# Turning a feed-forward layer's inputs on VectorE and through DRAM instead of on TensorE

## The chip, the core and the metric

The kernel runs on one core of a Trainium2 chip. TensorE (PE) multiplies matrices, VectorE (DVE) and ScalarE (ACT) work element by element, GpSimd (POOL) makes index tables and issues indirect DMAs, and SyncE (SP) issues the large DMAs. Each engine takes its instructions in order[...]. An engine waits on semaphores that other engines and DMAs raise. The metric is the device time of one execution in microseconds (us), taken as the median of several runs.

## What is computed

The input x has 4 x 512 = 2048 rows (tokens) of 512 numbers, in f32. Every token has a number that selects one of four experts, and every expert is one 512 x 512 matrix. The first half adds a gated expert product to x, the second half adds a gated feed-forward layer (FFN).

```
x = x + tanh(g_xattn) * moe(layernorm(x), ids, ctx, ctx, ctx)
x = x + tanh(g_ffn) * ffn(layernorm(x), w1, w3, w2, wr)

def moe(h, ids, Wg, Wu, Wd):          # E = 4
    expert = min(ids // 6250, 3)
    y_e = (silu(h @ Wg[e].T) * (h @ Wu[e].T)) @ Wd[e].T
    return y of the token's own expert

def ffn(h, w1, w3, w2, wr):
    gates = top 2 of softmax(h @ wr.T), normalised      # 8 routes
    h = silu(silu(h @ w1.T) @ w3.T) @ w2.T
    out = zeros_like(h)
    for k in range(2):
        out = out.at[index_k].add(gate_k * h)           # index_k is 0 to 7
    return out
```

The FFN's output lands in rows 0 to 7 of the result alone, since the indices of the routes, 0 to 7, are used as row numbers. All 2048 tokens contribute to these eight rows, so every token still goes through both FFN layers and the routing.

## The kernel before

**Tiles.** Tokens are sorted by expert on the chip. The sorted tokens make 17 passes of 128 rows: passes 0 to 12 (NF = 13) hold tokens of one expert, and passes 13 to 16 hold remainders, in four groups of Q = 32 rows with an expert for each group. `order` (L389) is the order in which passes are run: 0, 1, 2, 3, 4, 5, NF, 6, 7, 8, NF+1, 9, 10, NF+2, 11, 12, NF+3.

**One pass, first half.** `gather` (L393) fetches the rows of x with an indirect DMA on POOL. `load` (L436) reads the expert's number into a register on SP and issues the DMA of its matrix, 1 MB. A full pass loads one matrix, a remainder pass four. The matrices lie in the pool "mp" of seven buffers, so a load waits until the matrix seven places earlier in the order of loads has been used for the last time. `centre` (L403) takes mean and variance and subtracts the mean on DVE; `scale` (L409) makes the inverse root there. `turn_in` (L413) transposes the tile on PE (four transposes of 128 x 128) and ACT copies it out. `up` multiplies by the matrix (z, L459), with ACT's silu and DVE's product (g, L473) behind it. `turn_mid` transposes g, and `down` multiplies again (y, L459) and adds to x on DVE (L487); POOL scatters x to the output. `norms` (L498) normalises the new x for the FFN, into h_f.

**To the FFN.** `turn_out` (L516) transposes h_f on PE ("tp_f", four transposes), and ACT copies the result into `hT2`, one tile for each FFN half of 1024 tokens. A half of the FFN starts when its last pass is turned: `sums_of_hT` (L597) makes the logits of the routing for each half of 512 columns ("lg", L705, 64 small matmuls in all) and, on DVE, four sums T1 to T4 of the half's quarters; T1 is the difference of the two column halves. `turned` (L714) transposes the logits on DVE. `first_layer` then runs a scheme of seven block products in place of eight ("X", "Y", "Z", L628), and `second_layer` the product with w3 ("v", L736) and the gated sums.

**Order.** The order is written out by hand: the program's order is the order on each engine. The loop at L878 runs i from 2 to 18. An iteration puts on PE: `up` of order[i], `turn_in` of order[i+1], `down` of order[i-1], `turn_out` of order[i-2], a `step` of a running FFN, `turn_mid` of order[i]. It also issues `gather` and `load` of order[i+3]. FFN half 0 begins at the end of i = 10, because order[8] is pass 7.

**Start.** Before the first pass the kernel makes tables on DVE: `from_row` (rows to gather), `which0` and `matrix_table(0, 2)` (experts of the first two passes). The table for the other passes, `matrix_table(2, NU)`, and `row_tables` (L311) follow after the first two tiles are centred. `which1` (L847) is a copy on POOL behind the first gather, which makes the second load wait for that gather. PE runs 31 matmuls without a use ("idle", `busy`) during this time.

Of the kernel before, what the change touches and what calls it, by code (L numbers as in the profile page):

```python
# [25 lines left out]
def tile_gated_moe_ffn(  # L26
# [59 lines left out]
    xp = ctx.enter_context(tc.tile_pool(name="xp", bufs=5))  # L86
    work = ctx.enter_context(tc.tile_pool(name="work", bufs=3))
    small = ctx.enter_context(tc.tile_pool(name="small", bufs=4))
    ps_mm = ctx.enter_context(tc.tile_pool(name="ps_mm", bufs=2, space=bass.MemoryType.PSUM))
    ps_x = ctx.enter_context(tc.tile_pool(name="ps_x", bufs=2, space=bass.MemoryType.PSUM))  # L90
    ps_y = ctx.enter_context(tc.tile_pool(name="ps_y", bufs=1, space=bass.MemoryType.PSUM))
# [189 lines left out]
    later = ct_([P, 2 * E, NU], F32, "later")  # L281
    stepped = ct_([P, 2 * E - 1, NU], F32, "stepped")

    def matrix_table(n0, n1):
        n = n1 - n0
        nc.vector.tensor_tensor(
            later[:, :, n0:n1],
            place0[:, n0:n1].unsqueeze(1).to_broadcast([P, 2 * E, n]),
            cut[:, 1 : 2 * E + 1].unsqueeze(2).to_broadcast([P, 2 * E, n]),
            ALU.is_ge,  # L290
        )
        nc.vector.tensor_tensor(
            stepped[:, :, n0:n1],
            later[:, 0 : 2 * E - 1, n0:n1],
            steps.unsqueeze(2).to_broadcast([P, 2 * E - 1, n]),
            ALU.mult,
        )
        with nc.allow_low_precision("whole numbers below 4096"):
            nc.vector.tensor_reduce(
                which[:, n0:n1], stepped[:, :, n0:n1].rearrange("p e n -> p n e"), AX.X, ALU.add  # L300
            )

    busy(21)
    from_row = ct_([P, NP], I32, "from_row")
    nc.vector.tensor_scalar(from_row, tok, -1.0, 0.0, ALU.add, ALU.max)
    matrix_table(0, 2)

    first = ct_([P, NU - NF], I32, "first")
    to_row = ct_([P, NP], I32, "to_row")
# [1 line left out]
    def row_tables():  # L311

        pad = ct_([P, NP], F32, "pad")
        nc.vector.tensor_scalar(pad, tok, 1.0, float(4 * NT), ALU.is_lt, ALU.mult)
        nc.vector.scalar_tensor_tensor(to_row, tok, -1.0, pad, ALU.add, ALU.add)

        pads = ct_([P, E], F32, "pads")
        nc.vector.tensor_sub(pads, size[:, 2, :], num[:, 0, :])
        behind = ct_([P, E, NU - NF], F32, "behind")
        nc.vector.tensor_tensor(  # L320
            behind,
            later[:, E : 2 * E, NF:NU],
            pads.unsqueeze(2).to_broadcast([P, E, NU - NF]),
            ALU.mult,
        )
        psum = ct_([P, NU - NF], F32, "psum")
        nc.vector.tensor_reduce(psum, behind.rearrange("p e n -> p n e"), AX.X, ALU.add)
        nc.vector.tensor_sub(psum, place0[:, NF:NU], psum)
        nc.vector.tensor_scalar(
            first, psum, float(-(NB - 1) * TB), float(TB), ALU.add, ALU.min  # L330
        )


    hT2 = [ct_([P, KC, TB + (Q if b == NB - 1 else 0)], F32, f"hT2_{b}") for b in range(NB)]
    s1 = ct_([P, KC, TB], F32, "s1")
    acc = ps_acc.tile([P, D], F32, tag="acc", name="acc")
    accT = ps_acc.tile([P, KC, NR], F32, tag="acc", name="accT")
# [98 lines left out]
    def load(p):  # L436

        n0, n = (p, 1) if p < NF else (NF + (p - NF) * G, G)
        mats[p] = []
        for i in range(n0, n0 + n):  # L440
            at = nc.values_load(
                early[i] if i in early else which[0:1, i : i + 1],
                engines=[SP],
                min_val=0,
                max_val=(E - 1) * D,
                skip_runtime_bounds_check_because="an expert's number, times D",
            )
            m = mp.tile([P, KC, D], F32, tag="m", name=f"m_{i}")
            nc.sync.dma_start(m, ctxT[bass.ds(at, D), :].rearrange("(k p) f -> p k f", p=P))
            mats[p].append(m)  # L450
# [47 lines left out]
    def norms(p_in, p_out):  # L498
# [14 lines left out]
        if p_in is not None:  # L513
            rss[p_in] = rs[-1]

    def turn_out(p):  # L516

        tp = transposed(hs2.pop(p), f"f{p}").rearrange("p (k t) -> p k t", k=KC)
        if p < NF:
            b, t = divmod(p, TB // P)  # L520
            nc.scalar.copy(hT2[b][:, :, t * P : (t + 1) * P], tp)  # L521
            return
        for i in range(G):
            n = (p - NF) * G + i
            place = NF * P + n * Q - (NB - 1) * TB
            at = nc.values_load(
                first[0:1, n : n + 1],
                engines=[ACT],
                min_val=min(place - E * (Q - 1), TB),
                max_val=min(place, TB),  # L530
                skip_runtime_bounds_check_because="its place less at most E (Q - 1) pads, at most TB",
            )
            nc.scalar.copy(hT2[NB - 1][:, :, bass.ds(at, Q)], tp[:, :, i * Q : (i + 1) * Q])

    def route(b, lt):

# [60 lines left out]
    def sums_of_hT(b):  # L597


        lgs = [logits(b, half) for half in range(2)]  # L600
        b11, b12 = hT2[b][:, 0:2, 0:HB], hT2[b][:, 0:2, HB:TB]
        b21, b22 = hT2[b][:, 2:4, 0:HB], hT2[b][:, 2:4, HB:TB]
        ts = [ffp.tile([P, 2, HB], F32, tag=f"T{i}", name=f"T{i}_{b}") for i in range(1, 5)]
        nc.vector.tensor_sub(ts[0], b12, b11)
        lts[b] = [turned(b, half, lg) for half, lg in enumerate(lgs)]
        nc.vector.tensor_sub(ts[1], b22, ts[0])
        nc.vector.tensor_sub(ts[2], b22, b12)
        nc.vector.tensor_sub(ts[3], b21, ts[1])
        return b11, b21, b22, ts

    def first_layer(b):
# [14 lines left out]
        def product(out_ps, a, bb, c, start):  # L626
            for k in range(2):
                nc.tensor.matmul(  # L628
                    out_ps,
                    a[:, k, c * P : (c + 1) * P],  # L630
                    bb[:, k, :],
                    start=start and k == 0,
                    stop=k == 1,
                    skip_group_check=True,
                )
# [62 lines left out]
    def logits(b, half):  # L698


        lg = ps_x.tile([P, P], F32, tag="x", name=f"lg_{b}_{half}")
        for k in range(KC):
            cols = hT2[b][:, k, half * HB : (half + 1) * HB].rearrange("p (t c) -> p t c", t=TT)
            for i in range(P // Q):
                nc.tensor.matmul(  # L705
                    lg[i * Q : (i + 1) * Q, :],
                    wr[:, k, :],
                    cols[:, :, i * Q : (i + 1) * Q],
                    start=(k == 0),
                    stop=(k == KC - 1),  # L710
                )
        return lg
# [116 lines left out]

    SHORT = 1  # L830
    last = {b: max(i for i, p in enumerate(order) if min(p // (TB // P), NB - 1) == b) for b in range(NB)}
    running, hT_sums, lts, w1_sums = [], {}, {}, []

    def step():
        if running:
# [3 lines left out]
            if r in (0, SHORT):  # L839
                step()  # L840

    early = {order[0]: which0[0:1, :]}
    load(order[0])
    gather(order[0])

    which1 = ct_([P, 1], I32, "which1")
    nc.gpsimd.tensor_copy(which1[0:1, :], which[0:1, order[1] : order[1] + 1])  # L847
    early[order[1]] = which1[0:1, :]
    for i in range(1, 5):
        gather(order[i])  # L850
    load(order[1])
    nc.sync.dma_start(gates[:, 0:1], g_xattn.to_broadcast([P, 1]))
    nc.sync.dma_start(gates[:, 1:2], g_ffn.to_broadcast([P, 1]))
    first_in(order[0])
    centre(order[1])
    scale(order[0], order[1])
    matrix_table(2, NU)
    load(order[2])
    w1 = load_w(w1T, "w1")
    wr = load_w(wrT, "wr")  # L860
    load(order[3])
    row_tables()
    positions.close()
    ffp = ctx.enter_context(tc.tile_pool(name="ffp", bufs=1))
    up(order[0], inside=lambda: turn_in(order[1]))
    centre(order[2])
    scale(order[2])
# [5 lines left out]
    turn_mid(order[1])  # L873
    norms(order[3], order[0])
    load(order[4])
    summing = sums_of_w1()
    owed = []
    for i in range(2, NP + 2):  # L878
        if i < NP:
            up(order[i])  # L880
        if i + 1 < NP:
            turn_in(order[i + 1])
        if i + 2 < NP:
            centre(order[i + 2])
        if i + 3 < NP:
            gather(order[i + 3])
            load(order[i + 3])
        if i <= NP:
            down(order[i - 1])
        turn_out(order[i - 2])  # L890
        if i <= NP:
            norms(order[i + 2] if i + 2 < NP else None, order[i - 1])
        step()
        if i > NP:
            step()
        if 5 <= i < 9:
            next(summing)
        if i == 7:
            w3 = load_w(w3T, "w3")
            w2 = load_w(w2T, "w2")  # L900
        if i < NP:
            turn_mid(order[i])
        for b in range(NB):
            if last[b] == i - 2:
                hT_sums[b] = sums_of_hT(b)
                running.append(ffn(b))
        if last[0] != i - 2:
            step()
    fetched = False
    while running:  # L910
        step()
# [50 lines left out]
```

## Time and profile before

| | |
|---|---|
| time, median of three runs | 278.3 us (278.0 to 278.48) |
| the profiled execution | 278.8 us |
| its span, first to last instruction | 277.1 us |
| granted TensorE clock | 0.998 |
| four transposes "tp_f" of one turn_out, in the chain | 0.44 us |
| ACT copy of one turn_out (L521) | 586 ns |
| DVE transpose 128x128 of the logits (L716) | 304 ns |
| DVE 128x512 scalar_tensor_tensor (L473, L487) | 749 ns |
| moved by DMA | 42.54 MB, mean 154 GB/s |

The span is what the profiler sees of one execution, and the execution's own time is 1.7 us longer. Durations in the profile are those of this one execution. A line such as `109.60 3.57 PE y L459 x32` in the chain says: at 109.60 us from the start, for 3.57 us, PE ran 32 matmuls of line 459 that write y. A matmul of f32 appears as two instructions, so a full pass has 8 where the program has 4, and a remainder pass 32. "SPq" is the queue on which SP issues DMAs: the time beside it is that of the issue, not of the transfer. The trace leaves buffer numbers out of names (m, z, y), so passes are told apart by their time and their count of matmuls.

### The profile page before, as it was taken

The page shows a single profiled execution, that of the slowest core. Times are in us where ns is not written, and L with a number is a line of the kernel's source. Part 1 is how long each engine was busy: PE and PEld are TensorE (multiplying, and loading weights), DVE is VectorE, ACT ScalarE, POOL GpSimd, SP SyncE. Part 2 cuts the span into 40 slices and gives each one's busy share as a digit, 9 for nine tenths or more (in the row PEclk, how much of TensorE's full clock was granted, in tenths as well). Part 3 has the DMA queues.
Part 4 walks back from the last instruction along what each step waited for, and adds up shares of the span by engine and source line. Part 5 has one row for each costly group of instructions (what it writes and reads, how often), then busy time and mean ns, then how long its engine had stood idle before and what let it go on. Part 6 is the DMA issues. An engine that isn't in the chain of part 4 may idle for free.

```text
span 277.1 us, 3564 instructions
## 1 busy us (share of the span) xinstructions
PE 267.2 (96%) x1173; PEld 125.2 (45%) x1173; DVE 147.3 (53%) x596; ACT 69.2 (25%) x134; POOL 39.1 (14%) x62
## 2 busy tenths in 40 slices
PE   5888999999999999999999999999999999999994
PEld 2443555553454445444344344534345444444362
DVE  6369877777977769927354392516352620711000
ACT  2022222322322322124133132312113233311120
POOL 5510122221222102311110010101010000000000
PEclk9999999999999999999999999999999999999999
DMA  0775999656759998498305085001000000000000
GB/s 1 231 260 202 383 391 392 237 195 222 222 181 392 393 392 323 139 384 275 145 10 180 2 289 200 38 0 40 1 11 2 0 0 1 0 0 2 0 0 2
DMA packets 20722, 42.54 MB, mean 154 GB/s; under 512 B 2143, under 2 KB 2207, under 8 KB 20704
## 3 DMA queue, kind: packets, MB, share of 16 engines
q1 hardware_dynamic: 17952, 33.66, 34.4%
q0 software_dynamic: 2720, 8.65, 8.7%
q8 instruction: 9, 0.15, 0.2%
q14 instruction: 9, 0.07, 0.1%
q10 hardware_dynamic: 32, 0.01, 0.0%
HBM read 38.10 MB, written 4.47 MB: 154 GB/s over the span
## 4 chain that ended last, share of the span: by engine, by line
PE 91%; DVE 4%; DMA 3%; issue 1%; POOL 0%; DVEq 0%
PE y L459 21%; PE v L736 20%; PE z L459 19%; PE X L628 10%; PE Y L628 5%; PE tp_f L386 3%; PE tp_g L386 3%; PE tp_a L386 3%; PE Z L628 2%; DMA x<-in_x_dram,from_row 2%; PE acc L748 1%; PE lg L705 1%; PE accT L764 1%; DMA idt<-in_ids_dram 1%; PE o L820 0%
## 5 line engine op out<-in xcount | busy, mean ns | idle before, releaser
L459 PE MATMUL z<-m,hT 128*32 128x512 f32 (+1 forms) x232 | 61.8, 595 | 0.2 <-ACT hT L434 0.2
L459 PE MATMUL y<-m,gT 128*32 128x512 f32 (+1 forms) x232 | 61.4, 594 | 0.0
L736 PE MATMUL v<-w,s 128*128 128x512 f32 (+1 forms) x136 | 57.3, 570 | 0.0
L736 PEld LDWEIGHTS v<-w,s 128*128 128x128 f32 x136 | 25.0, 190 | 27.2 <-issue 26.7
L459 PEld LDWEIGHTS z<-m,hT 128*32 128x32 f32 (+1 forms) x232 | 22.6, 146 | 29.4 <-issue 28.1
L459 PEld LDWEIGHTS y<-m,gT 128*32 128x32 f32 (+1 forms) x232 | 22.6, 146 | 27.8 <-issue 27.8
L488 POOL DMA_INDIRECT out_dram<-x,to_row x17 | 17.2, 1010 | 87.6 <-DVE x L487 85.4
L395 POOL DMA_INDIRECT x<-in_x_dram,from_row x17 | 16.8, 989 | 76.2 <-DVE h_a L407 36.1
L473 DVE SCALAR_TENSOR_TENSOR g<-z,rs_a,g 128x512 f32<-128x512 f32 x17 | 12.7, 749 | 25.7 <-ACT g L472 25.7
L472 ACT ACTIVATE g<-z,rs_a 128x512 f32<-128x512 f32 x17 | 11.7, 688 | 51.2 <-PE z L459 50.7
L487 DVE SCALAR_TENSOR_TENSOR x<-y,tg,x 128x512 f32<-128x512 f32 x17 | 12.7, 749 | 17.3 <-PE y L459 17.3
L744 ACT ACTIVATE s<-v 128x512 f32<-128x512 f32 (+1 forms) x17 | 9.7, 572 | 41.9 <-PE v L736 41.9
L521 ACT COPY hT<-tp_f 128x512 f32<-128x512 f32 x13 | 7.6, 586 | 43.5 <-PE tp_f L386 43.5
L346 DVE BATCH_NORM_STATS2 st_a<-x 128x6 f32<-128x512 f32 x16 | 11.0, 688 | 9.9 <-DMA x<-in_x_dram,from_row 9.9
L628 PE MATMUL X<-T,S 128*128 128x512 f32 x32 | 15.0, 592 | 0.0
L386 PEld LDWEIGHTS tp_f<-ident,h_f 128*128 128x128 f32 x68 | 8.2, 141 | 10.2 <-issue 10.2
L386 PEld LDWEIGHTS tp_a<-ident,h_a 128*128 128x128 f32 x64 | 7.6, 141 | 10.2 <-issue 9.6
L346 DVE BATCH_NORM_STATS2 st_f<-x 128x6 f32<-128x512 f32 x17 | 11.8, 695 | 0.6
L479 ACT COPY gT<-tp_g 128x512 f32<-128x512 f32 x17 | 10.0, 586 | 8.0 <-PE tp_g L386 8.0
L646 DVE TENSOR_TENSOR s<-X,c 128x512 f32<-128x512 f32 x4 | 2.8, 692 | 16.2 <-PE X L628 16.2
L386 PE MATMUL tp_g<-ident,g 128*128 128x128 f32 x68 | 10.2, 273 | 1.0 <-DVE g L473 1.0
L386 PEld LDWEIGHTS tp_g<-ident,g 128*128 128x128 f32 x68 | 8.2, 141 | 5.5 <-issue 5.2
(164 smaller groups left out, 273.4 us busy)
## 6 DMA issues: line engine op xcount, KB each, us to landing
m<-in_ctxT_dram SPq DMA_DIRECT2D x29, 1024.0 KB
w<-in_w1T_dram SPq DMA_DIRECT2D x1, 1024.0 KB
w<-in_w3T_dram SPq DMA_DIRECT2D x1, 1024.0 KB
w<-in_w2T_dram SPq DMA_DIRECT2D x1, 1024.0 KB
x<-in_x_dram,from_row POOLq DMA_INDIRECT x17, 6.1
out_dram<-x,to_row POOLq DMA_INDIRECT x17, 6.1
wr<-in_wrT_dram SPq DMA_DIRECT2D x1, 64.0 KB
x_first<-out_dram SPq DMA_DIRECT2D x4, 4.0 KB
```

The lines of the kernel that those rows point to most:

```text
L346: nc.vector.bn_stats(st, xt)
L386: nc.tensor.transpose(tp[:, k * P : (k + 1) * P], h[:, k * P : (k + 1) * P], ident)
L395: nc.gpsimd.indirect_dma_start(out=xt, out_offset=None, in_=x, in_offset=bass.IndirectOffsetOnAxis(ap=from_row[:, p : p + 1], axis=0),)
L459: nc.tensor.matmul(out_ps[i * n : (i + 1) * n, :], lhs[:, k * P + i * n : k * P + (i + 1) * n], m[:, k, :], start=(k == 0), stop=(k == KC ...
L472: nc.scalar.activation(g, z, AF.Silu, scale=rs)
L473: nc.vector.scalar_tensor_tensor(g, z, rs, g, ALU.mult, ALU.mult)
L479: nc.scalar.copy(gT, tp)
L487: nc.vector.scalar_tensor_tensor(xt, y, tg[:, 0:1], xt, ALU.mult, ALU.add)
L488: nc.gpsimd.indirect_dma_start(out=out, out_offset=bass.IndirectOffsetOnAxis(ap=to_row[:, p : p + 1], axis=0), in_=xt, in_offset=None, bou ...
L628: nc.tensor.matmul(out_ps, a[:, k, c * P : (c + 1) * P], bb[:, k, :], start=start and k == 0, stop=k == 1, skip_group_check=True,)
L736: nc.tensor.matmul(v, s1[:, k, c_b + t * P : c_b + (t + 1) * P], w3[:, k, c0 : c0 + n], start=(k == 0), stop=(k == KC - 1),)
L744: nc.scalar.activation(s2, v, AF.Silu)
```

## The change

Passes 0 to 11 are no longer transposed on PE. Four of them make a set. `set_turned` transposes each 32x32 block of h_f on DVE and writes it to the set's own tile (`hT2[b]`, now one tile for each set, and one for the rest). After the fourth pass of a set, SP issues a DMA that copies the tile, 1 MB, to a buffer in DRAM. `fetch_turned`, called one iteration later, issues four DMAs of 256 KB that read it back, so that each block comes to the partitions of its column; columns are then in another order within the set. Passes 12 to 16 keep the transposes on PE. `set_turned` and `fetch_turned` stand behind `norms` in the loop. FFN half 0 begins one iteration later, at the end of i = 11, and a `step` now follows each iteration without the old exception.

The tables are made in one piece, and all of them ahead of the first gather in the program's order. `held` takes the place of `which1`: POOL copies the experts' numbers to it in two parts, one behind the first gather and one behind the fifth, and the loads read it. `scale(order[0])` stands ahead of `centre(order[1])`. The two loads of gates move behind the third matrix, and w1 and wr are loaded at i = 2.

```diff
-    def matrix_table(n0, n1):
...
-    matrix_table(0, 2)
+    nc.vector.tensor_tensor(
+        later,
+        place0.unsqueeze(1).to_broadcast([P, 2 * E, NU]),
+        cut[:, 1 : 2 * E + 1].unsqueeze(2).to_broadcast([P, 2 * E, NU]),
+        ALU.is_ge,
+    )
...
-    hT2 = [ct_([P, KC, TB + (Q if b == NB - 1 else 0)], F32, f"hT2_{b}") for b in range(NB)]
+    NS = NF // 4 * 4
+    assert NS == (NB * 2 - 1) * TT and E * (Q - 1) <= NF * P - NS * P
+    hT2 = [ct_([P, G, KC, P], F32, f"hT2_{b}") for b in range(NB * 2 - 1)]
+    hT2.append(ct_([P, KC, HB + Q], F32, "hT2_last"))
+
+    def inputs(b):
+        if b < NB * 2 - 1:
+            return hT2[b].rearrange("p g k c -> p k g c")
+        return hT2[b][:, :, 0:HB].rearrange("p k (g c) -> p k g c", g=TT)
...
+    def set_turned(p):
+        b, i = divmod(p, 4)
+        place = hT2[b]
+        h = hs2.pop(p)
+        nc.vector.transpose(
+            place.rearrange("p q k (i t) -> p k q i t", i=4)[:, :, :, i, :],
+            h.rearrange("p (k q t) -> p k q t", k=KC, q=4),
+        )
+        if i == 3:
+            copy = dram.tile([P, 4, KC * P], F32, tag=f"copy{b}", name=f"copy_{b}")
+            nc.sync.dma_start(copy, place.rearrange("p q k c -> p q (k c)"))
+            turning.append((place, copy))
+
+    def fetch_turned():
+        for place, copy in turning:
+            for q in range(4):
+                nc.sync.dma_start(
+                    place[q * Q : (q + 1) * Q].rearrange("f g k c -> f g (k c)"),
+                    copy[:, q, :].rearrange("(g f) c -> f g c", g=4),
+                )
+        turning.clear()
...
-        b11, b12 = hT2[b][:, 0:2, 0:HB], hT2[b][:, 0:2, HB:TB]
-        b21, b22 = hT2[b][:, 2:4, 0:HB], hT2[b][:, 2:4, HB:TB]
+        left, right = inputs(2 * b), inputs(2 * b + 1)
+        b11, b12, b21, b22 = left[:, 0:2], right[:, 0:2], left[:, 2:4], right[:, 2:4]
...
-            cols = hT2[b][:, k, half * HB : (half + 1) * HB].rearrange("p (t c) -> p t c", t=TT)
+            cols = inputs(2 * b + half)[:, k]
...
     row_tables()
     positions.close()
     ffp = ctx.enter_context(tc.tile_pool(name="ffp", bufs=1))
+    held = ct_([P, NU], I32, "held")
...
+    load(order[0])
+    gather(order[0])
+    one = slice(order[1], order[1] + 1)
+    nc.gpsimd.tensor_copy(held[0:1, one], which[0:1, one])
+    load(order[1])
+    for i in range(1, 5):
+        gather(order[i])
+    rest = slice(order[1] + 1, NU)
+    nc.gpsimd.tensor_copy(held[0:1, rest], which[0:1, rest])
+    first_in(order[0])
+    scale(order[0])
+    centre(order[1])
+    scale(order[1])
+    load(order[2])
+    nc.sync.dma_start(gates[:, 0:1], g_xattn.to_broadcast([P, 1]))
+    nc.sync.dma_start(gates[:, 1:2], g_ffn.to_broadcast([P, 1]))
+    load(order[3])
...
     load(order[4])
+    fetch_turned()
+    set_turned(order[0])
...
-        turn_out(order[i - 2])
+        if order[i - 2] >= NS:
+            turn_out(order[i - 2])
         if i <= NP:
             norms(order[i + 2] if i + 2 < NP else None, order[i - 1])
+            fetch_turned()
+            if order[i - 1] < NS:
+                set_turned(order[i - 1])
         step()
...
+        if i == 2:
+            w1 = load_w(w1T, "w1")
+            wr = load_w(wrT, "wr")
...
         for b in range(NB):
-            if last[b] == i - 2:
+            if last[b] + 2 + (b == 0) == i:
                 hT_sums[b] = sums_of_hT(b)
                 running.append(ffn(b))
-        if last[0] != i - 2:
-            step()
+        step()
```

More of the change, by code (lines that the diff above doesn't have):

```diff
@@ L88, in tile_gated_moe_ffn @@
     small = ctx.enter_context(tc.tile_pool(name="small", bufs=4))
+    dram = ctx.enter_context(tc.tile_pool(name="dram", bufs=1, space=bass.MemoryType.DRAM))
     ps_mm = ctx.enter_context(tc.tile_pool(name="ps_mm", bufs=2, space=bass.MemoryType.PSUM))
@@ L282, in tile_gated_moe_ffn @@
     stepped = ct_([P, 2 * E - 1, NU], F32, "stepped")
-    def matrix_table(n0, n1):
[L285 to L301, printed above, removed]
     busy(21)
@@ L305, in tile_gated_moe_ffn @@
     nc.vector.tensor_scalar(from_row, tok, -1.0, 0.0, ALU.add, ALU.max)
-    matrix_table(0, 2)
+    nc.vector.tensor_tensor(
[4 more added lines that the diff above has]
+    )
+    nc.vector.tensor_tensor(
+        stepped,
+        later[:, 0 : 2 * E - 1],
+        steps.unsqueeze(2).to_broadcast([P, 2 * E - 1, NU]),
+        ALU.mult,
+    )
+    with nc.allow_low_precision("whole numbers below 4096"):
+        nc.vector.tensor_reduce(which, stepped.rearrange("p e n -> p n e"), AX.X, ALU.add)
     first = ct_([P, NU - NF], I32, "first")
@@ L329, in row_tables @@
         nc.vector.tensor_scalar(
-            first, psum, float(-(NB - 1) * TB), float(TB), ALU.add, ALU.min
+            first, psum, float(-NS * P), float(HB), ALU.add, ALU.min
         )
-    hT2 = [ct_([P, KC, TB + (Q if b == NB - 1 else 0)], F32, f"hT2_{b}") for b in range(NB)]
+    NS = NF // 4 * 4
[6 more added lines that the diff above has]
+        return hT2[b][:, :, 0:HB].rearrange("p k (g c) -> p k g c", g=TT)
     s1 = ct_([P, KC, TB], F32, "s1")
@@ L441, in load @@
             at = nc.values_load(
-                early[i] if i in early else which[0:1, i : i + 1],
+                look_up(i),
                 engines=[SP],
@@ L514, in norms @@
             rss[p_in] = rs[-1]
+    def set_turned(p):
[16 more added lines that the diff above has]
+                    copy[:, q, :].rearrange("(g f) c -> f g c", g=4),
+                )
+        turning.clear()
     def turn_out(p):
@@ L519, in turn_out @@
         if p < NF:
-            b, t = divmod(p, TB // P)
-            nc.scalar.copy(hT2[b][:, :, t * P : (t + 1) * P], tp)
+            t = p - NS
+            nc.scalar.copy(hT2[-1][:, :, t * P : (t + 1) * P], tp)
             return
@@ L524, in turn_out @@
             n = (p - NF) * G + i
-            place = NF * P + n * Q - (NB - 1) * TB
+            place = (NF - NS) * P + n * Q
             at = nc.values_load(
@@ L528, in turn_out @@
                 engines=[ACT],
-                min_val=min(place - E * (Q - 1), TB),
-                max_val=min(place, TB),
-                skip_runtime_bounds_check_because="its place less at most E (Q - 1) pads, at most TB",
+                min_val=min(place - E * (Q - 1), HB),
+                max_val=min(place, HB),
+                skip_runtime_bounds_check_because="its place less at most E (Q - 1) pads, at most HB",
             )
-            nc.scalar.copy(hT2[NB - 1][:, :, bass.ds(at, Q)], tp[:, :, i * Q : (i + 1) * Q])
+            nc.scalar.copy(hT2[-1][:, :, bass.ds(at, Q)], tp[:, :, i * Q : (i + 1) * Q])
     def route(b, lt):
@@ L600, in sums_of_hT @@
         lgs = [logits(b, half) for half in range(2)]
-        b11, b12 = hT2[b][:, 0:2, 0:HB], hT2[b][:, 0:2, HB:TB]
-        b21, b22 = hT2[b][:, 2:4, 0:HB], hT2[b][:, 2:4, HB:TB]
-        ts = [ffp.tile([P, 2, HB], F32, tag=f"T{i}", name=f"T{i}_{b}") for i in range(1, 5)]
+        left, right = inputs(2 * b), inputs(2 * b + 1)
+        b11, b12, b21, b22 = left[:, 0:2], right[:, 0:2], left[:, 2:4], right[:, 2:4]
+        ts = [
+            ffp.tile([P, 2, TT, P], F32, tag=f"T{i}", name=f"T{i}_{b}") for i in range(1, 5)
+        ]
         nc.vector.tensor_sub(ts[0], b12, b11)
@@ L630, in product @@
                     a[:, k, c * P : (c + 1) * P],
-                    bb[:, k, :],
+                    bb[:, k],
                     start=start and k == 0,
@@ L831, in tile_gated_moe_ffn @@
     last = {b: max(i for i, p in enumerate(order) if min(p // (TB // P), NB - 1) == b) for b in range(NB)}
-    running, hT_sums, lts, w1_sums = [], {}, {}, []
+    running, hT_sums, lts, w1_sums, turning = [], {}, {}, [], []
     def step():
@@ L840, in step @@
                 step()
[L842 to L861, printed above, removed]
     row_tables()
@@ L864, in tile_gated_moe_ffn, with look_up @@
     ffp = ctx.enter_context(tc.tile_pool(name="ffp", bufs=1))
+    held = ct_([P, NU], I32, "held")
+    def look_up(i):
+        return which0[0:1, :] if i == order[0] else held[0:1, i : i + 1]
+    load(order[0])
[15 more added lines that the diff above has]
+    load(order[3])
     up(order[0], inside=lambda: turn_in(order[1]))
```

## The prediction, made before the changed kernel was run

> **What bounds the kernel now.** I read the page first. Part 1 gives PE 267.2 of 277.1 us, and part 4 puts 91% of the chain that ended last on PE.
>
> ```profile
> PE 267.2 (96%) x1173; PEld 125.2 (45%) x1173; DVE 147.3 (53%) x596; ACT 69.2 (25%) x134; POOL 39.1 (14%) x62
> ...
> PE   5888999999999999999999999999999999999994
> ...
> DMA  0775999656759998498305085001000000000000
> ```
>
> So the time is PE's queue end to end, and any gap in it is lost. PE idles only before 23.3 us. Next, the chain in order of time around the place where the first FFN half begins:
>
> ```profile
> 102.78 0.44 PE tp_f L386 x4
> 103.21 0.44 PE tp_g L386 x4
> 103.65 1.88 PE lg L705 x64
> 105.53 3.63 PE z L459 x8
> 109.16 0.44 PE tp_a L386 x4
> 109.60 3.57 PE y L459 x32
> 113.17 0.59 PE tp_f L386 x4
> 113.76 1.72 PE X L628 x4
> ```
>
> A turn_out costs PE 0.435 us (four transposes, "tp_f"). The y of 32 matmuls that ends at 113.17 is pass NF+1, which holds four expert matrices. Third, the timeline of SP's queue, the only issuer of the large loads:
>
> ```profile
> 81.52 2.62 SPq L115 DMA_DIRECT2D w<-in_w3T_dram  x1
> 84.18 2.45 SPq L115 DMA_DIRECT2D w<-in_w2T_dram  x1
> ...
> 102.81 0.37 SPq L449 DMA_DIRECT2D m<-in_ctxT_dram  x1
> ...
> 113.18 3.15 SPq L449 DMA_DIRECT2D m<-in_ctxT_dram  x4
> ```
>
> SP issues one load at 102.81 and the next four only at 113.18, 0.01 us after NF+1's y: the pool "mp" has seven buffers, and these four wait for NF+1's. The wait view of SP says the same: 99.7 us in 11 waits for y of L459, the longest 14.4. Last, the busy windows (columns: PE, PEld, DVE, ACT, POOL, PE clock, DMA share, GB/s):
>
> ```profile
> 104.00:108.00 4.00, 4.00 (x63) 2.51 (x55) 3.90 (x23) 0.33 (x1) 1.96 (x2) 1.00 1.06 389
> 108.00:112.00 4.00, 4.00 (x31) 1.50 (x33) 4.00 (x6) 1.17 (x2) 0.00 (x0) 1.00 0.42 161
> 112.00:113.00 1.00, 1.00 (x12) 0.13 (x4) 1.00 (x2) 0.00 (x0) 0.87 (x1) 1.00 0.00 0
> ```
>
> The DMA engines are full from about 80 to 109.6 us at some 390 GB/s, empty at 112, and full again behind the four loads.
>
> [...]w3's issue took 2.62 us, with four loads of 1 MB ahead, against 0.37 for a lone load.[...]the first ten "idle" matmuls took 4.00 us, the later 21 took 4.70.[...]
>
> **The change part by part.**
>
> *Transposes off PE.* The built order of the changed kernel has 5 turn_outs for 17, so the change does what it says: 12 x 0.435 = 5.2 us off PE's path. ACT loses 12 copies of 586 ns, which bound nothing.
>
> *Transposes on DVE.* A 128x512 block transpose is not in the trace. L716 takes 304 ns for 128 columns; scalar_tensor_tensor grows from 350 ns (L920) to 749 from 128 to 512 columns, so I take 0.304 + 0.399 = 0.70 us. Below: it must stream 512 columns, so not under 0.5 (the cheap subtract of L407 takes 0.49). Above: its writes are scattered runs of 32, say three times, 2.1 us. DVE's iteration in the first phase is: x to the end of h_f 4.2 us (36.50 to 40.70), g 0.8, centre 1.4, together 6.4; with 0.7 it is 7.1, and 7.8 where w1's sums (0.69) fall. PE's becomes 3.44 + 0.44 + 3.44 + 0.44 = 7.76. g is done about 6.1 us after the y before it, and PE wants it at 7.8, so DVE hides this. At 2.1 us it would not.
>
> *Tables ahead.* DVE now makes the tables (0.38 + 0.35 + 0.51 + 1.43 us for row_tables) before the first centre. from_row ends at 8.86 and the gather goes 0.28 later, as before; the tables end at about 11.5, x lands at 12.58. They cost nothing. Their old place, 19.87 to 22.43, held g back: tp_g waited 0.99 us until 23.32. Now scale(0) runs while x of tile 1 is on its way, g is done at about 21.0, and tp_g starts when PE's queue reaches it, at 22.33: **-1.0 us**. What is late next is PE itself. If x of tile 1 lands later, the gain shrinks, to zero at worst; I see no larger loss. SP gets m of tile 2 at about 15.6, not 21.68; the gates go behind it and w1 and wr to i = 2; all are early.
>
> *Copies, set 0 and set 2.* SP waits for DVE before each copy, with the next m behind it, but that m itself waits for a later y: nothing. Their fetches have two iterations or more until logits ask for them: nothing.
>
> *Copy and fetch of set 1* (tiles 4 to 7). Here the order on SP's queue is:
>
> ```
> DMACopy copy_1<-hT2_1 [waits DVE]
> DMACopy m_21 [waits PE]
> DMACopy m_22 [waits PE]
> DMACopy m_23 [waits PE]
> DMACopy m_24 [waits PE]
> DMACopy hT2_1<-copy_1 (four of them)
> ```
>
> and on PE: y of NF+1, tp_g, lg of half 0, lg of half 1, the last waiting for all four fetches. m_22 to m_24 are three of the four loads that the trace shows at 113.18. So the fetch can't be issued before NF+1's y ends,[...] and PE wants it 1.4 us after that same y. This is the wait that decides. Its price:
>
> 1. NF+1's y ends at 113.17 - 1.0 (start) - 8 x 0.435 (turn_outs up to there) - 2.07 (logits now behind it: 1.88, and z 3.63 for 3.44) = 106.6. PE reaches lg of half 1 at 106.6 + 0.44 + 0.94 = 108.0.
> 2. In the trace the engines serve the nine loads issued from 77.81 on, with the tiles' gathers and scatters, from 80.0 to 109.6. Now these are issued 1.0 + 5 x 0.435 = 3.2 us earlier: 76.8 to 106.4. copy_1 (1.05 MB, released about 96, while they are full) adds 2.7: 109.1. So m_22 to m_24 join a queue that still runs. Without the backlog it would be 106.6 + 0.9 before data flow.
> 3. m_22 to m_24 and one gather and one scatter (0.26 MB each) are 3.67 MB: 9.4 us, 118.5.
> 4. The fetch, 1.05 MB: 2.7 us at 390 GB/s[...]: it lands at 123.3.
> 5. DVE then makes T1 (1.22), and turned (0.30) must free the bank that X needs, with hops: X starts at about 125.2, lg of half 1 hidden beside it. In the trace X starts at 113.76: 11.4 later.
> 6. PE has stood for 15 us[...]. I take 1.5 us, between 0 and 3.
> 7. Off again: tp_g before X is already done (-0.44), three turn_outs are still to be saved (-1.31). PE is full from here, so nothing makes up for the gap.
>
> Sum: 277.1 + 11.4 - 0.4 - 1.3 + 1.5 = 288.3 us span. The profiled execution took 278.8, so 1.7 lies around the span: 290.0. The median is 0.5 below that execution: **289.5 us**.
>
> *FFN one iteration later.* Steps only change places on a PE that is full; at i = 18 one more v (3.44 us) stands before the second half's logits, which is cover, not cost. Nothing.
>
> **The rivals.**
>
> *A shorter stall.* The backlog is gone before 106.6, the fetch runs at 390 GB/s and the clock stays up: 106.6 + 0.9 + 8.1 (3.15 MB) + 2.7 + 0.6 = 118.9, X at 120.8, 277.1 + 7.0 - 1.7 = 282.4, median 283.8. For it: the engines do run empty at 112 now. Against it: copy_1 is new, and everything comes earlier, PE more than the DMA.
>
> *DVE becomes the bound as well.* At 2.1 us a block transpose makes DVE's iteration 8.5 against 7.76; after its slack of 1.6 that is some 4.5 us until NF+1's y (111). The backlog is gone then:[...] X at 129.0: 277.1 + 15.2 - 1.7 + 1.5 = 292.1, median 293.3. For it: the destination is strided. Against it: DVE's other strided outputs show no such price.
>
> *Faster: the fetch doesn't wait.* One mechanism: the fetch of set 1 lands before PE asks for it, because m_22 to m_24 find free buffers earlier than at NF+1's y. Then the gains stand alone: 278.3 - 5.2 - 1.0 = 272.1. The point from which it decides: T1 and turned take 1.9 us after the landing, so landing at about 112.5 gives back the gain of 6.2. For it: set 0 and set 2 do have the room. Against it: SP's four issues 0.01 us after that y, and the built order.
>
> **How the numbers follow.** Forecast 0.66, shorter stall 0.12, DVE as well 0.11, faster 0.11. All but the last are slower. Within the forecast the fetch's rate (2 us), the clock (3 us) and the backlog (2 us) make 286 to 293; to leave out no more than 2 in 10 I take 284 to 293.5. 0.2% (0.56 us) is about what a measurement of this kernel can tell from no change: faster 0.10, the same 0.02, slower 0.88.
>
> **What would show it.** Right: PE idle for some 15 us before lg of half 1, ended by a DMA into hT2; DMA full through it, and SP's three m issues just ahead of the four fetches; slower matmuls just after; tp_g at about 22.3 us; DVE transposes of about 0.7 us. Wrong: no such gap, or one ended by DVE; m loads issued before NF+1's y ends; the fetch ahead of m_22 to m_24 in time.

## The result, and the profile after

The changed kernel takes 296.58 us (median of 4 runs, 295.5 to 299.5), the kernel before 278.39 us (278.0 to 279.26). It is 18 us slower; the ratio taken over the runs is 1.0676, with a 95% interval of 1.0644 to 1.0709 (that of the two medians is 1.065). The forecast was slower, at 289.5 us, with a range that ended at 293.5.

The page of the changed kernel (span, part 1, and two rows of part 2):

```profile
span 294.8 us, 3485 instructions
...
PE 265.1 (90%) x1125; PEld 121.2 (41%) x1125; DVE 155.9 (53%) x605; ACT 63.3 (21%) x122; POOL 39.3 (13%) x63
...
PE   5899999999998890079997999999999999999994
...
PEclk9999999999999997569999999999999999999999
```

PE is busy 2.1 us less than before (265.1 for 267.2), but idle 29.7 us where it was 9.9. The row of PE shows where: two slices at 0, and the clock's row drops to 5 just there. What PE waited for (columns: total us, times, longest):

```profile
PE lg L740 <- DMA hT<-copy: 16.6, 1, 16.6
PE cnt L194 <- DVE hot L191: 3.0, 1, 3.0
PE X L663 <- DVE s L681: 1.7, 1, 1.7
PE z L465 <- DMA m<-in_ctxT_dram: 1.3, 1, 1.3
PE tp_a L439 <- DVE h_a L434: 1.2, 1, 1.2
PE tp_g L392 <- DVE g L479: 1.2, 1, 1.2
PE z L465 <- ACT s L779: 0.5, 1, 0.5
```

One wait of 16.6 us is for a DMA from "copy" into hT2, ahead of the logits. The third, fourth, sixth and seventh lines, 4.7 us together, are new too (X, z, tp_g and z again; the wait of tp_g for g that the kernel before had at 22 us is gone). SP's queue around it:

```profile
97.80 0.35 SPq L537 DMA_DIRECT2D copy<-hT  x1
99.61 11.60 SPq L455 DMA_DIRECT2D m<-in_ctxT_dram  x4
111.30 2.07 SPq L543 DMA_DIRECT2D hT<-copy  x4
114.08 42.67 SPq L455 DMA_DIRECT2D m<-in_ctxT_dram  x3
```

The copy of set 1 is issued at 97.80. The second line merges four loads: one at 99.61 and three that SP issued from 108.98 to 111.21, at the end of NF+1's y (105.39 + 3.69 = 109.08 in the chain). Only then came the fetches. The chain of waits goes on from there:

```profile
112.87 14.21 DMA hT<-copy
127.08 0.14 issue
127.21 1.93 PE lg L740 x32
129.15 2.84 PE X L663 x4
131.98 1.72 PE Z L663 x4
```

The last fetch was issued at 112.87 and seen at 127.08. The first X after the gap takes 2.84 us, the Z after it 1.72 for the same four matmuls. The windows (columns as in the prediction) show what the DMA engines did meanwhile:

```profile
114.00:120.00 6.00, 0.00 (x0) 0.00 (x0) 0.00 (x0) 0.00 (x0) 0.78 (x1) 0.50 0.99 358
120.00:121.00 1.00, 0.00 (x0) 0.00 (x0) 0.00 (x0) 0.00 (x0) 0.20 (x1) 0.50 1.09 391
121.00:126.00 5.00, 0.00 (x0) 0.00 (x0) 0.00 (x0) 0.00 (x0) 0.00 (x0) 0.50 1.07 217
```

First the three matrices and tiles of x at 358 to 391 GB/s, then five microseconds at 217: 1.09 MB, about the size of the fetch (1.05 MB). All 16 engines count as busy in both. PE's clock is 0.50 throughout.

### The profile page after: what moved, and what is told of

It reads as the page before. It is cut to its first block, busy times and chain, and to the rows that moved or that the text cites. A ratio compares the mean times of both kernels' runs of the same rounds, so it can differ in the third digit from the quotient of the medians.

```text
span 294.8 us, 3485 instructions
## 1 busy us (share of the span) xinstructions
PE 265.1 (90%) x1125; PEld 121.2 (41%) x1125; DVE 155.9 (53%) x605; ACT 63.3 (21%) x122; POOL 39.3 (13%) x63
## 4 chain that ended last, share of the span: by engine, by line
PE 78%; DMA 12%; DVE 6%; issue 1%; SPq 1%; ACT 0%; DVEq 0%
PE z L465 19%; PE y L465 18%; PE v L771 17%; PE X L663 9%; DMA m<-in_ctxT_dram 6%; DMA hT<-copy 5%; PE Y L663 4%; PE Z L663 2%; PE tp_a L392 2%; PE tp_g L392 2%; PE acc L783 1%; PE lg L740 1%; DMA x<-in_x_dram,from_row 1%; PE tp_f L392 1%; PE accT L799 1%
## 5 line engine op out<-in xcount | busy, mean ns | idle before, releaser
L493 DVE SCALAR_TENSOR_TENSOR x<-y,tg,x 128x512 f32<-128x512 f32 x17 | 12.7, 748 | 16.7 <-PE y L465 16.6
L740 PE MATMUL lg<-hT,wr 128*32 128x128 f32 x96 | 4.1, 324 | 16.6 <-DMA hT<-copy 16.6
L740 PEld LDWEIGHTS lg<-hT,wr 128*32 128x32 f32 x96 | 3.1, 129 | 17.8 <-issue 17.8
L422 ACT COPY hT<-tp_a 128x512 f32<-128x512 f32 x16 | 9.3, 579 | 3.1 <-PE tp_a L392 3.1
```

Source lines behind the costliest of these rows:

```text
L493: nc.vector.scalar_tensor_tensor(xt, y, tg[:, 0:1], xt, ALU.mult, ALU.add)
L740: nc.tensor.matmul(lg[i * Q : (i + 1) * Q, :], wr[:, k, :], cols[:, :, i * Q : (i + 1) * Q], start=(k == 0), stop=(k == KC - 1),)
```

## The experiments

Each is compared with the kernel before on the same chip. All are edits of the changed kernel, but for e4.

**e1: the fetch ahead of the loads.**

```diff
+        fetch_turned()
         if i + 3 < NP:
             gather(order[i + 3])
             load(order[i + 3])
...
-            fetch_turned()
             if order[i - 1] < NS:
```

> Edit: in each iteration the fetch stands ahead of that iteration's matrix loads on SP's queue; all else as in the changed kernel. Theory A (the fetch of set 1 is stuck on SP behind three loads that wait for NF+1's y[...]): the fetch waits only for its copy, lands at about 112.5 us in place of 127.1, PE's gap before the second logits falls from 16.6 to 2 to 3 us and the half clock goes; about 281 us. Theory B (the DMA engines are simply too full, the order on SP does not matter): the gap stays over 10 us, time over 290.

Measured: ratio 1.0177 (1.0142 to 1.0212), 283.84 us. The wait before the logits fell from 16.6 to 4.8 us, for an edit of the order on SP alone. So theory A holds for most of the gap. (The profiled execution, at 285.99 us, was the slowest of five.) But it stayed above the forecast of 2 to 3 us. The chain of e1 says why:

```profile
97.03 9.98 DMA copy<-hT
...
108.41 7.24 DMA hT<-copy
115.65 0.14 issue
115.79 1.93 PE lg L740 x32
117.72 3.71 PE X L663 x4
```

The copy took 10.0 us to land, with w3, w2 and matrices issued ahead of it, and the fetch 7.2 us after its last issue, where step 4 of the sum had 4.8. From 110 to 114 us the engines moved 219 to 221 GB/s, while they counted as full. Theory B is right in part: full engines delay the copy, as e7 will show.

**e2: FFN half 0 one iteration later again.**

```diff
-            if last[b] + 2 + (b == 0) == i:
+            if last[b] + 2 + 2 * (b == 0) == i:
```

> Edit: FFN half 0 begins one iteration later again (end of i = 12); SP's order untouched. Theory A: the fetch lands at the same moment (about 127), but PE has up, down and two or three transposes of one more pass (about 8.2 us) to do first: the gap falls from 16.6 to about 8.4 us, about 288 us. Theory B gives the same gap here; it is e1 that tells the two apart. Theory C (the gap is a fixed price of the copy and fetch themselves, counted from when PE asks): the gap stays at 16 us.

Measured: 287.69 us, one run; the wait is 9.3 us and ends at 127.09, as in the changed kernel (127.21). The landing is fixed by SP's queue and not by when PE asks: theory C falls.

**e3: set 1 not fetched.**

```diff
-            for q in range(4):
+            for q in range(0 if place is hT2[1] else 4):
```

> Leaves out the four fetches of set 1, so that this set's columns are block transposes only. All waits for the landing go, the copy's traffic stays. Theory A: no gap before the second logits and no half clock: 296.6 - 16.6 - 0.6 (DVE's T1 behind the landing) - 1.9 (clock) = about 277.5 us, with the smaller gaps (g at 90, matrix of pass 9 at 100, s at 160) still there. If more than 3 us of the loss lies elsewhere, it stays above 281.

Measured: 283.45 us, one run; not 277.5. The kernel leaves out these four fetches, so it serves for its times alone. The expectation failed, and with it the idea that the fetch is the only cause. PE's wait has another name, and DVE's timeline at this place says what stands ahead (small instructions of norms left out):

```profile
PE X L663 <- DVE lt L751: 5.1, 1, 5.1
```

```profile
110.12 0.75 DVE L493 SCALAR_TENSOR_TENSOR x<-y,tg,x 128x512 f32<-128x512 f32 x1
...
113.76 0.54 DVE L517 TENSOR_SCALAR h_f<-x,mv_f,rs_f 128x512 f32<-128x512 f32 x1
114.22 1.22 DVE L639 TENSOR_TENSOR T<-hT,hT 128x1024 f32<-128x1024 f32 x1
115.35 0.51 DVE L751 STREAM_TRANSPOSE lt<-lg 128x128 f32<-128x128 f32 x2
```

X needs the bank that the logits hold until `turned` has read them, and on DVE `turned` stands behind NF+1's x and norms (4.2 us) and T1. The kernel before skipped the step in the iteration in which FFN half 0 began, so a whole pass of PE work lay between. The change dropped this exception. In the changed kernel these 5.1 us lie under the wait for the fetch.

**e4: the start alone.** The kernel before, with the changed start (the tables in one piece, as in the change).

```diff
-    matrix_table(0, 2)
...
+    scale(order[0])
     centre(order[1])
-    scale(order[0], order[1])
-    matrix_table(2, NU)
+    scale(order[1])
```

> The kernel before, with only the start of the changed kernel: tables in one piece ahead of the first tile, held, scale before centre, w1 and wr loaded at i = 2. All turn_outs on PE. Forecast's term: 1.0 us less than before, about 277.3 us. Rival: what is gained ahead of 22 us is lost to later transfers, about 278.3.

Measured: ratio 0.9967 (0.9953 to 0.9982), that is 0.5 to 1.3 us of 278.36; the medians lie 0.65 us apart. The first tp_g starts at 22.34 us and no longer waits for g. The term of 1.0 us holds, within this interval.

**e5: the exception kept.**

```diff
-        step()
+        if i != 11:
+            step()
```

> Edit: the changed kernel, with no step in the iteration in which FFN half 0 begins (the exception that the kernel before had and the change removed). The fetch is as late as before. Theory D (the removed exception is a second cause, hidden under the first: X must wait for DVE, whose T1 and turned stand behind norms, and it also shifts the FFN's steps against the iterations, so that sums s stand behind norms): PE's 1.7 us before X at 160 and 0.5 us before z at 195 go, the 16.6 us gap stays; 296.6 - 2.2 = about 294.4 us. Rival: those small gaps come from the block transpose on DVE (0.71 us each) and stay; 296.6.

Measured: 293.11 us, one run, span 291.4 for 294.8. PE's waits of this kernel:

```profile
PE lg L740 <- DMA hT<-copy: 16.0, 1, 16.0
PE cnt L194 <- DVE hot L191: 3.0, 1, 3.0
PE tp_g L392 <- DVE g L479: 1.7, 1, 1.7
```

The waits of X for s (1.7) and of z for s (0.5) are gone, with DVE's block transposes still there: theory D holds for these two, and the rival falls. Without the exception the FFN's steps are shifted by one against the iterations, and sums that X must wait for come behind norms on DVE. The span fell by 3.4 us, more than these 2.2: z's wait for pass 9's matrix (1.3) is missing too, and the wait for g is longer, both at a place that the edit doesn't touch. The small waits ahead of 105 us thus differ from one execution to the next.

**e6: e1, a later start and the exception together.**

```diff
-            if last[b] + 2 + (b == 0) == i:
+            if last[b] + 2 + 2 * (b == 0) == i:
...
-        step()
+        if i != 12:
+            step()
```

> Edit: e1 (fetch ahead of the loads), FFN half 0 begins at the end of i = 12, and no step in that iteration. Theories A and D together: the fetch lands near 115.6 us as in e1 and PE asks near 117, X stands behind one more pass; no gap before logits or X. Left are z for its matrix (1.7) and g (up to 1.4), and of the forecast's gains all: about 278.4 - 1.0 - 5.2 + 2 = 274 us. If A or D is wrong a gap of 5 us or more stays: 279 or more.

Measured: ratio 1.0186 (1.0142 to 1.0231), 285.04 us; not 274. The waits for the fetch and for `turned` are gone (0.9 us of idle inside the logits has no releaser named), but a new one has come:

```profile
PE z L465 <- DMA m<-in_ctxT_dram: 4.8, 3, 2.7
```

Two of the three, 3.3 us, are NF+2's z at 124 to 127, and its matmuls then crawl: 26 of them took 5.61 us, for 32 in 3.64 elsewhere. With the fetch ahead and the FFN's first X and Z behind, these three matrices are the late ones: the fetch is in the queue ahead of them, and in e1 the engines moved only 219 to 221 GB/s during it. So the loss was moved, not removed: theory B again.

**e7: w3 and w2 later.** e6 with `if i == 11` for `if i == 7` ahead of the loads of w3 and w2. Theory E is that these 2 MB, issued ahead of pass 9's matrix and of the copy, delay both, and the gathers of x too.

> e6, with w3 and w2 loaded at i = 11 in place of i = 7, behind the matrices of NF+2 and pass 11. Theory E[...]: the waits for a matrix (1.3 to 1.7) and for g (1.2 to 1.4) go, and the copy lands some 5 us earlier; about 271.8 us. Rival: those waits come from DVE's extra 0.7 us a pass, and stay; as e6.

Measured: ratio 0.9946 (0.9918 to 0.9974), 277.89 us; not 271.8. The fetch is issued at 100.19 in place of 106.24, 3.9 us after its copy, and the wait of pass 9's z is gone. So theory E holds for the copy and for this matrix. For g it is not shown: e1 and e6, with w3 and w2 in their old place, have no wait for g either. One wait of 2.7 us for NF+2's matrices is left, with slow matmuls behind it.

**e8 and e12: set 1 on PE.** Sets 0 and 2 go the new way, passes 4 to 7 are turned on PE, and FFN half 0 starts as before. e12 is the same kernel again. (Left out of the diff: `turn_out` copies these four passes to set 1's tile.)

```diff
...
-        if order[i - 2] >= NS:
+        if order[i - 2] >= NS or 4 <= order[i - 2] < 8:
             turn_out(order[i - 2])
...
-            if last[b] + 2 + (b == 0) == i:
+            if last[b] + 2 == i:
...
-        step()
+        if i != 10:
+            step()
```

> Edit: the changed kernel with set 1 (passes 4 to 7) turned on PE as before, sets 0 and 2 through DVE and DRAM, and FFN half 0 at the end of i = 10 with no step there, as before. Theory A: nothing waits for a copy; 278.4 - 0.7 (start, as e4 measured) - 8 x 0.435 = about 274.3 us. If the other sets' copies or DVE's transposes cost PE time too, 276 or more.

> The kernel of e8 once more, on the same chip as e11 and with more rounds: 0.983 as before. It does 16 transposes (1.7 us of PE) more than e11 and has no copy to wait for at FFN half 0. If e11's waits are all gone it is 1.7 us slower than e11; if not, it is the faster.

Measured: e8 0.983 (0.9786 to 0.9874), e12 0.9863 (0.983 to 0.9896). In both PE waits for no copy, and the waits at 90 and 100 us are absent, with w3 and w2 where the change has them. What is left at this place is 0.4 us in e8 and 1.4 in e12, for g and s on DVE. With 8 of 12 turns moved this way the change is a gain of 1 to 2%.

**e9: all mended.** e1, the exception at i = 11, w3 and w2 at i = 11.

> The changed kernel with three edits: the fetch ahead of the loads (e1), no step in the iteration in which FFN half 0 begins (e5), w3 and w2 loaded at i = 11 (e7). FFN half 0 begins at i = 11 as in the change, so that its X and Z stand ahead of NF+2's z and give its matrices 7 us more than in e6 and e7. Theories A, D and E together: the fetch is issued near 100 as in e7 and lands near 106.5, PE asks near 108; no gap over 1 us; PE's busy time about 263 and the start's idle 5 to 6: about 272.5 us where before takes 278.4, ratio 0.979. If the DMA engines simply carry too much at this place (theory B), a gap for NF+2's matrices or for the fetch of 3 us or more stays, and the ratio is over 0.99.

Measured: ratio 0.9901 (0.9859 to 0.9942), 275.2 us; not 272.5. One wait is left: 2.3 us before the second logits, and slow matmuls behind it. The table of waits names no releaser, but the chain leads from these logits back to the fetch, seen at 109.39; the 1.3 us from there to the logits at 110.70 have no cause in the profile. NF+2's matrices are in time. (The profiled execution, at 277.31 us, was one of the two slowest of six.)

**e10: the fetch of set 2 on two queues.**

```diff
-            for q in range(4):
-                nc.sync.dma_start(
+            for q in (0, 2, 1, 3) if place is hT2[2] else range(4):
+                eng = nc.scalar if place is hT2[2] and q > 1 else nc.sync
+                eng.dma_start(
```

> e9, with the fetch of set 2 split: quarters 0 and 1 (partitions 0 to 63) issued by SP, 2 and 3 (64 to 127) by ACT. Set 2's fetch has the DMA engines almost to itself, so its rate can be read. [...]1.05 MB at up to 400 GB/s, 2.6 us, where the four in one queue ran at 218. Rival[...]: 218 stays.

Inconclusive (276.45 us, one run). SP issued its two at 173.81, ACT its two only at 176.39, so the halves came one after the other, and no microsecond of this stretch moved more than 256 GB/s. Whether the two halves at once go faster stays open.

**e11: the logits behind one more z.** With e9's places for the fetch and for w3 and w2.

```diff
+        if i == 12:
+            hT_sums[0] = sums_of_hT(0)
+            running.append(ffn(0))
         fetch_turned()
...
-            if last[b] + 2 + (b == 0) == i:
+            if b == 1 and last[b] + 2 == i:
```

> e9 with sums_of_hT and the start of FFN half 0 put into i = 12 between turn_in and down, so that z and four transposes of one more pass (3.9 us) stand ahead of the logits, and X still ahead of NF+2's z. If the 2.35 us before the second logits in e9 are only the rest of the fetch's time at 218 GB/s (it landed at 110.6, PE asked at 108.3), the gap and the half clock behind it go and nothing takes their place: span about 271 us, ratio to before 0.977. If PE idles elsewhere instead (g or s behind T1 to T4 on DVE), it stays at 0.985 or more.

Measured: ratio 0.9874 (0.9842 to 0.9906). The wait before the logits is gone, so what PE lacked there in e9 was time. A wait of 1.4 us of NF+2's z for s on DVE is new, as the second half of the expectation had it. Beside e12 on the same chip (0.9863) the two can't be told apart.

## Why the prediction was right in direction and wrong in size

The mechanism that it named is the one that the runs show: e1 and e2 tie the gap to SP's order, and the built order of the queues, which the prediction read, gave it in full. The measured time lies 7.1 us above the forecast, and 3.1 above the range. Two things failed: the landing of the fetch (steps 1 to 4), put at 123.3 and measured at 127.1, and the term "FFN one iteration later ... Nothing", which cost 2.2 us. By the steps of the sum:

- *Steps 1 and 2, the end of NF+1's y and the backlog:* y was put at 106.6 and ended at 109.1. Two new waits of PE ahead of it are as long as that: 1.2 us for g at 90 and 1.3 us for the matrix of pass 9 at 100. Step 2 had the engines full until 109.1, and step 1 let PE come 4.5 us earlier, but no step asked whether what comes through these full engines would still be in time. For the matrix e7 shows that moving w3 and w2 takes the wait away; for g the cause stays open. The backlog that was to cover a late y ended at about 107.8, and the engines ran empty:

```profile
108.00:110.00 2.00, 2.00 (x36) 0.99 (x32) 1.93 (x4) 0.36 (x1) 0.00 (x0) 1.00 0.10 39
110.00:112.00 2.00, 0.56 (x23) 0.29 (x12) 1.90 (x12) 0.23 (x1) 1.52 (x2) 1.00 0.72 269
```

So the three matrices flowed from about 110.0, not from 109.1: 0.9 us late. With y at 106.6 they would have joined the backlog; the late y cost some 2 us, an estimate from 107.8 and 110.0.
- *Step 3, the three matrices and two tiles:* put at 9.4 us, took 11.0 (110.0 to 121.0): 131 GB/s in the first microsecond, in which SP was still issuing, and 370 behind it, for 390. 1.6 us late.
- *Step 4, the fetch:* the 4.8 us from 118.5 to the landing were my estimate, and no trace of before shows such a transfer. It moved at 217 GB/s (121 to 126 us), not at 390; the cause of this rate is not shown. It took 6.1 us from 121.0 to the landing at 127.1, for 4.8: 1.3 us late.
- *Step 5, X:* forecast 1.9 us behind the landing, measured 2.1 (127.08 to 129.15).
- *Step 6, the clock:* forecast 1.5; X took 2.84 for 1.72, so 1.1 us. The 1.5 was my estimate: in the trace of before the mean granted clock is 0.998, and only the first "idle" matmuls are slow (0.40 us each, for 0.22 later). In this gap the granted clock is 0.50 from 3.3 us into it, and full again 3.8 us after PE has resumed (0.50 from 113.9 to 131.0 us).
- *Step 7:* as forecast; four turn_outs stand behind X, where the kernel before has seven.
- *"FFN one iteration later ... Nothing":* wrong. It cost 2.2 us (1.7 before X, 0.5 before z), which e5 takes away. PE is full, but its steps wait for DVE, and the dropped exception put these sums behind norms. This is the step that failed in kind; the others failed in size.

The errors add up: 3.9 us of X's lateness, 2.2 for the steps, less 0.4 for the clock, give 5.7 of the 6.5 us by which the span was missed (294.8 for 288.3). The rest, 0.8 us, I did not trace.

Of the rest, the start was right (1.0 forecast, 0.5 to 1.3 in e4; tp_g at 22.34 there and at 21.88 in the changed kernel, for 22.33). The block transpose was right: 12 of them took 712 ns each, for 0.70. DVE as a bound did not come about: it was busy 53% of the span. That this rival put X at 129.0, where it was measured at 129.15, is chance; it had y at 111. (The median of the shorter stall should be 283.6 by its own sum, not 283.8.) The rival "faster" was wrong in one more way: it let the gains stand alone once the fetch was early, and e3 shows a floor under it. Without any fetch PE still waits 5.1 us, for `turned` behind norms. The 0.88 on slower was right for a reason only half seen.

## What to carry to other kernels

In this kernel a transfer issued behind others on one queue inherited their wait: PE stood for 16.6 us, and for 4.8 once the fetch was ahead of the loads (e1). Put a transfer where its own input is ready, and ask what then becomes late in its place (in e6, NF+2's matrices: 3.3 us). When a bound engine gets faster, go through every load that it meets and ask which is now late, also those that the change doesn't touch. An odd exception in a hand-written order ("no step in this iteration") can be the cover of a wait: before it is dropped, look on the other engine for what it hides.

## What the runs showed of the hardware that was not expected

Four fetches of 256 KB, each to 32 partitions and issued one behind the other, ran at 217 GB/s (121 to 126 us of the changed kernel), while the engines counted as fully busy; just before (120 to 121 us), with loads to 128 partitions on the same queue, they moved 391. In e1 it was the same (219 to 221 from 110 to 114 us). A gap of 2.3 us in e9 was followed by the half clock: the granted clock was 0.69 in the mean from 110 to 112 us (PE resumed at 110.70), 0.50 from 112 to 114 and 0.96 from 114 to 116, and the eight matmuls of z there took 4.49 us, where eight took 3.60 in the pass before. In e7, 26 matmuls behind a gap of 2.7 us took 5.17 us, where 32 took 3.64 elsewhere. A block transpose that writes runs of 32 numbers scattered over the tile took 712 ns for 512 columns, where 128 columns took 304 in the kernel before and the estimate for a plain output was 700.
